# Two attention stages rebuilt: half steps, two PSUM rings, a mask product on TensorE

## The chip, the cores and the metric

The kernel runs as one program on one core of a Trainium2 chip. The metric is the time of one execution on the device in microseconds, lower is better. A profiled execution gives the trace from which the stages are read; its engines are PE (TensorE products), PEld (its weight loads), DVE (VectorE), ACT (ScalarE), POOL (GpSimd) and SP (the queue that issues most DMAs).

## What is computed

The input is eight sequences of 512 tokens with 128 features, in fp32. Twelve blocks follow one another, each with a residual connection and a layer norm in front: an LSTM-like block, a state-space mixer, the LSTM-like block again; a mixture of experts, attention L1, the mixture again; a gated block with rounded weights, a recurrence, the gated block again; a ReLU block, attention L3, the ReLU block again. This case is about the two attentions. Both have 16 heads of 8 features; L3 is causal:

```python
scores = jnp.einsum('bhqk,bhsk->bhqs', q, k) / jnp.sqrt(jnp.float32(dk))
causal_mask = jnp.triu(jnp.ones((s, s), dtype=bool), k=1)      # L3 alone
scores = jnp.where(causal_mask, jnp.float32(-1000000000.0), scores)
weights = jax.nn.softmax(scores, axis=-1)
ctx = jnp.einsum('bhqs,bhsk->bhqk', weights, v)
```

L1 adds position features to the normalized input ahead of the projections, adds that sum to its output, and normalizes once more with gamma and beta.

## The kernel before

Every stage works sequence by sequence; the eight sequences of x stay in SBUF for the whole run. `_run_stages` (L1307) calls the twelve stages in order. Within a stage the program text gives each engine its order, except where the scheduler of the tile framework moves instructions that are ready earlier; waits come from tiles: a tile of a ring with n buffers can be written again once the reader of the one n before it is done.

An attention stage (`attention`, L1002) is a pipeline over sequences:

- `project` (L1065): layer norm (statistics on DVE, the root on POOL, the application on ACT, L263), transposes, the products for q and k, each split in two fp32r halves (lead on ACT, trail on DVE), the products for v, and eight pairs of "spread" products that put the 8 features and both halves of a head on 32 rows: qT and kT of head group g hold four heads, 32 rows each.
- `maxima` (L1119): for each chunk c of 128 queries, each group and each head a product of 32 rows into one bank of the ring "mm" (three banks), whose negated row maximum DVE takes (L1146). In L3 a custom DVE instruction (L1135) adds the mask while it takes the maximum. 64 products and 64 DVE instructions per sequence. The maxima are then transposed and split in two halves (mT).
- `weighted` (L1168): 16 steps per sequence, one for each group g and chunk c of 128 keys. A step makes four products of keys by queries (32 rows each, scores transposed), and four more that add the negated maximum (max_rows by mT) in the same banks: two tiles of two banks, scores0 and scores1, one buffer each. ACT takes the exponential of each tile (L1223, 128 x 1024 values); in L3 the ranges are shorter (queries from chunk c on), and POOL clears what is above the diagonal in the first 128 queries (L1225). The value sums of the step before follow on PE: four products of 32 columns in one bank, "av", which fill the group's sums over its four chunks; v has a column of ones, so that the sum of weights comes with it.
- `fill` (L1162): products of zeros by ones into the bank of value sums, that add nothing: one per step in L1, c + 1 per step in L3.
- `attended` (L1241): transposes of the four ctx tiles, division, the output product, residual and (L1) the second norm, again applied on ACT.

In `weighted`, each step yields twice (room 3, then 2), and the loop at L1052 puts in between: `attended` of the sequence before, `project` of the next, then up to five maxima of the next sequence per step until they are done. The first sequence is projected and has its maxima taken ahead of all steps; the last one has none beside it. A stage begins with its constants (spread, zeros, ones, max_rows, mask, L1018 to L1039) and its weights, which `self.load(key)` (L1012) fetches on the SP queue into a tile that the mixer stage used before.

PSUM has eight banks: three of "mm", four of scores, one of "av". "mm" also serves all projections, transposes and output products.

Of the kernel before, what the change touches and what calls it, by code (L numbers as in the profile page):

```python
# [207 lines left out]

class _Kernel:
# [34 lines left out]
    def norm(self, x, pool, out=None, tag="xn", scalar=False):  # L244
# [26 lines left out]
        return xn  # L271

# [61 lines left out]
    def l0_attn(self):  # L334
# [8 lines left out]
        with ExitStack() as s:  # L343
# [58 lines left out]
            for _ in self.mixer_out(NB - 1):  # L402
                pass

# [216 lines left out]
    def l1_ffn(self):  # L621
# [3 lines left out]
        with ExitStack() as s:  # L625
# [3 lines left out]
            self.spread = keep.tile([P, 8, P], F32R, name="spread")  # L629
            nc.vector.tensor_copy(  # L630
                self.spread.rearrange("p e m -> p (e m)"), self.w["moe", "spread"]
# [4 lines left out]
            for b in range(NB):  # L636
                ahead = self.routed(b + 1) if b + 1 < NB else iter(())
                for _ in self.experts(b):
                    next(ahead, None)
                for _ in ahead:  # L640
                    pass
# [33 lines left out]
    def experts(self, b):  # L675
# [12 lines left out]
        for e in range(9):  # L688
# [7 lines left out]
            if e < 8:  # L696
                if e % 2 == 0:
                    pw = []
                    for k in range(e, e + 2):
                        r = bass.ts(k % 4, 32)  # L700
                        pw.append(ps.tile([P, L], F32, name="pw"))
                        self.mm(pw[-1], self.spread[r, k, :], q["shareT"][r, :])
                nc.vector.tensor_tensor(act, act, pw[e % 2], ALU.mult)  # L703
# [297 lines left out]

    def attention(self, key, causal):  # L1002
# [7 lines left out]

        nc, tc = self.nc, self.tc
        self.load(key)  # L1012
        with ExitStack() as s:
            keep = s.enter_context(tc.tile_pool(name="keep", bufs=1))
            sb = s.enter_context(tc.tile_pool(name="sb", bufs=2))
            ps = s.enter_context(tc.tile_pool(name="ps", bufs=3, space=bass.MemoryType.PSUM))
            self.key, self.causal, self.sb, self.ps = key, causal, sb, ps
            spread = keep.tile([P, 2, 2, 4, P], F32R, name="spread")  # L1018
            nc.gpsimd.memset(spread.bitcast(F32), 0.0)
            for g in range(4):  # L1020
                r = bass.ts(g, 32)
                nc.vector.tensor_copy(
                    spread[r, :, :, g, :],
                    self.w["heads", "spread"][r, :].rearrange("p (w h m) -> p w h m", w=2, h=2),
                )
            self.zeros = keep.tile([P, P], BF16, name="zeros")
            nc.gpsimd.memset(self.zeros, 0.0)
            self.ones = keep.tile([P, L], BF16, name="ones")
            nc.gpsimd.memset(self.ones, 1.0)
            max_rows = keep.tile([P, 4, P], F32R, name="max_rows")  # L1030
            nc.vector.tensor_copy(
                max_rows, self.w["heads", "max_rows"].unsqueeze(2).to_broadcast([P, 4, P])
            )
            self.spread, self.max_rows = spread, max_rows
            if causal:
                self.mask = keep.tile([P, L], F32, name="mask")
                nc.gpsimd.memset(self.mask, 0.0)
                nc.gpsimd.tensor_copy(self.mask[:, L - P :], self.w["const", "mask_qk"])
                self.unread = keep.tile([P, L], F32, name="unread")  # L1039
            self.seqs = [{} for _ in range(NB)]  # L1040
            for _ in self.project(0):
                pass
            for _ in self.maxima(0):
                pass
            for b in range(NB):
                between = []
                if b > 0:
                    between.append((self.attended(b - 1), False))
                if b + 1 < NB:
                    between.append((self.project(b + 1), False))  # L1050
                    between.append((self.maxima(b + 1), True))
                for room in self.weighted(b):  # L1052
                    if between:
                        gen, small = between[0]
                        for _ in range(room if small else 2):
                            if next(gen, gen) is gen:
                                between.pop(0)
                                break
                for gen, _ in between:
                    for _ in gen:  # L1060
                        pass
            for _ in self.attended(NB - 1):
                pass

    def project(self, b):  # L1065

        nc, sb, ps, key = self.nc, self.sb, self.ps, self.key
        w = lambda n: self.w[key, n]
        q = self.seqs[b]
        xn = self.norm(self.x[b], self.ln_pool, scalar=True)  # L1070
        if key == "l1a":
            xp = sb.tile([P, NC, D], F32, name="xp", bufs=3)
            nc.gpsimd.tensor_tensor(xp, xn, w("pe").rearrange("p (c d) -> p c d", c=NC), ALU.add)
            q["xp"] = xp
        else:
            xp = xn
        yield
        xT = self.transposed(xp, ps, sb.tile([P, L], F32, name="xT"), nc.scalar.copy)
        yield
        halves = {}  # L1080
        for n in ("q", "k"):
            pq = ps.tile([P, L], F32, name="mm")
            self.mm(pq, w("w" + n), xT)
            lead = sb.tile([P, L], F32R, name=f"{n}_lead", bufs=1)
            nc.scalar.activation(lead, pq, AF.Identity, bias=w("b" + n))
            trail = sb.tile([P, L], F32R, name=f"{n}_trail", bufs=1)
            nc.vector.scalar_tensor_tensor(
                trail, pq, w("b" + n), lead.bitcast(F32), ALU.add, ALU.subtract
            )
            halves[n] = (lead, trail)  # L1090
            yield
        v = sb.tile([P, NC, 9 * 16 + 23], F32, name="v")
        q["v"] = v
        nc.gpsimd.memset(v, 1.0)
        pv = ps.tile([P, NC, P], F32, name="mm")
        for c in range(NC):
            self.mm(pv[:, c, :], xT[:, bass.ts(c, P)], w("wv"))
        for c in range(NC):
            nc.vector.tensor_tensor(
                v[:, c, :144].rearrange("p (h e) -> p h e", e=9)[:, :, 0:8],  # L1100
                pv[:, c, :].rearrange("p (h e) -> p h e", h=16),
                w("bv").rearrange("p (h e) -> p h e", h=16),
                ALU.add,
            )
        yield
        q["qT"], q["kT"] = [], []
        for g in range(4):
            r = bass.ts(g, 32)
            for which, n in enumerate(("q", "k")):
                pq = ps.tile([P, L], F32, name="mm")  # L1110
                self.mm(pq, self.spread[:, which, 0, g, :], halves[n][0], stop=False)
                self.mm(pq, self.spread[:, which, 1, g, :], halves[n][1], start=False)
                t = sb.tile([P, L], F32R, name=f"{n}T{g}")
                nc.scalar.copy(t, pq)
                q[n + "T"].append(t)
            if g % 2:
                yield

    def maxima(self, b):  # L1119

        nc, sb, ps, causal = self.nc, self.sb, self.ps, self.causal
        q = self.seqs[b]
        mx = sb.tile([P, NC, 4, 4], F32, name="max")
# [207 lines left out]
```

## Time and profile before

| what | value |
|---|---|
| median of three runs | 2760.23 us (2742.91 to 2765.81) |
| the profiled execution | 2768.8 us, span 2767.0 us |
| L1 attention, first exponential to last sequence's start | 862 to 1362 us |
| L3 attention, the same | 2189 to 2650 us |
| mean granted TensorE clock | 0.892 |

The profile page gives for each engine the time in which it was busy, the span in 40 slices with the granted clock, and the costliest groups of instructions. A group's row holds line, engine and operation, output and inputs by tile name with shapes, then the count, busy time, mean duration in ns, and the idle time of that engine just before, with what ended it. A PE instruction counts as busy from issue to a modelled end, so starts are better to reckon with than ends. The busy times by stretch hold busy time and, in brackets, instructions of each engine. The timeline merges like instructions that follow one another; "[0.54 <-PE mm L242]" is 0.54 us of idle time that ended when that product was done. L242 is the line of the helper through which nearly all products go, so tiles tell them apart. An fp32 product is recorded as two instructions of two passes each; fp32r and bf16 products are one pass.

### The profile page before, as it was taken

How to read it: one execution, taken by the hardware profiler on the slowest of the kernel's cores; microseconds unless marked ns; L12 is line 12 of the kernel's file. 1: busy time of each engine (PE TensorE's matmuls, PEld its weight loads, DVE VectorE, ACT ScalarE, POOL GpSimd, SP SyncE). 2: the span in 40 equal slices, each digit the busy share in tenths (PEclk: the TensorE clock that was granted, in tenths of full speed). 3: DMA queues.
4: the chain of work that ended last, by engine and by line, in shares of the span. 5: the costliest groups of instructions: out<-in, count | busy, mean ns of one | idle time of the engine just before them, and what ended most of it. 6: DMA issues, size and time to landing. Idle time of an engine off the chain costs nothing.

```text
span 2767.0 us, 32181 instructions
## 1 busy us (share of the span) xinstructions
PE 2336.9 (84%) x10995; PEld 1110.9 (40%) x11087; DVE 1706.9 (62%) x4623; ACT 1334.9 (48%) x2247; POOL 644.4 (23%) x926
## 2 busy tenths in 40 slices
PE   7588998889989888888879996752779998999999
PEld 3434444434434333333334443431544444444434
DVE  4565654577767566666627777848863556656621
ACT  3288775323334665555543333474435244444444
POOL 1123233021120111111111114544542122222220
PEclk9598888999987999999989998975979699989989
DMA  3000000000000000000000000000000000000001
GB/s 106 0 1 1 1 1 12 9 1 0 1 0 1 1 1 1 1 1 1 1 6 0 1 1 1 1 1 0 1 1 1 0 1 1 1 1 1 1 1 31
DMA packets 10051, 13.20 MB, mean 5 GB/s; under 512 B 416, under 2 KB 8736, under 8 KB 9760
## 3 DMA queue, kind: packets, MB, share of 16 engines
q1 hardware_dynamic: 7776, 10.11, 1.1%
q8 instruction: 87, 1.43, 0.2%
q10 hardware_dynamic: 2112, 1.05, 0.1%
q14 instruction: 76, 0.62, 0.1%
HBM read 9.06 MB, written 2.10 MB: 4 GB/s over the span
## 4 chain that ended last, share of the span: by engine, by line
PE 60%; DVE 21%; ACT 8%; POOL 7%; issue 4%; DMA 0%; DVEq 0%; ACTq 0%; POOLq 0%; SPq 0%
PE mm L242 15%; PE av L242 10%; PE po L242 8%; DVE max L1146 6%; PE pg L242 5%; PE pu L242 5%; PE ck L242 4%; DVE unread L1135 3%; PE scores L242 3%; PE ph L242 2%; POOL xn_rstd L257 1%; PE pw L242 1%; ACT e L1223 1%; PE mm L277 1%; DVE xn L268 1%
## 5 line engine op out<-in xcount | busy, mean ns | idle before, releaser
L1223 ACT ACTIVATE e<-scores 128x1024 f32<-128x1024 f32 (+3 forms) x512 | 417.9, 863 | 310.3 <-PE scores L242 196.0
L242 PE MATMUL mm<-kT,qT 32*128 32x512 f32 (+3 forms) x1024 | 383.7, 479 | 71.8 <-DVE max L1146 29.4
L1146 DVE TENSOR_REDUCE max<-mm 128x1 f32<-128x512 f32 x512 | 315.4, 684 | 105.6 <-PE mm L242 102.1
L1135 DVE CUSTOM_DVE_ANT_0 unread<-mm,mask 128x512 f32<-128x512 f32 (+3 forms) x512 | 251.8, 492 | 158.5 <-PE mm L242 89.6
L242 PEld LDWEIGHTS mm<-kT,qT 32*128 32x128 f32 x1024 | 166.9, 198 | 289.5 <-DVE max L1146 153.1
L242 PE MATMUL av<-e,v 128*32 128x512 f32 (+3 forms) x2048 | 263.2, 539 | 1.8 <-issue 1.8
L242 PE MATMUL scores<-qT,kT 32*128 32x512 f32 (+3 forms) x1024 | 183.9, 438 | 13.3 <-ACT e L1223 10.0
L694 ACT ACTIVATE act<-pg 128x512 f32<-128x512 f32 x144 | 86.0, 597 | 220.9 <-PE pg L242 196.7
L1225 POOL TENSOR_SCALAR_AFFINE_SELECT e<-e 128x256 f32<-128x256 f32 x256 | 102.2, 406 | 294.0 <-ACT e L1223 291.5
L278 ACT COPY xT<-mm 128x512 f32<-128x512 f32 x112 | 65.2, 584 | 209.2 <-PE mm L277 205.2
L242 PE MATMUL po<-act,w_moe 128*128 128x512 f32 x288 | 159.0, 637 | 0.6 <-DVE act L703 0.6
L242 PE MATMUL pg<-xT,w_moe 128*128 128x512 f32 x288 | 155.7, 624 | 0.0
L242 PE MATMUL scores<-mT,max_rows 32*128 32x512 f32 (+3 forms) x1024 | 150.7, 385 | 0.0
L242 PE MATMUL pu<-xT,w_moe 128*128 128x512 f32 x288 | 149.2, 600 | 0.0
L695 DVE TENSOR_TENSOR act<-act,pu 128x512 f32<-128x512 f32 x144 | 98.3, 683 | 55.6 <-PE pu L242 53.6
L257 POOL TENSOR_TENSOR xn_rstd<-xn_rs,nhalf 128x4 f32<-128x4 f32 x96 | 104.3, 1088 | 87.1 <-ACT xn L263 53.9
L242 PE MATMUL av<-ones,zeros 128*128 128x512 bf16 x356 | 118.7, 414 | 5.3 <-issue 5.3
L1148 POOL COPY copies<-max 128x128 f32<-128x128 f32 x64 | 18.6, 291 | 448.9 <-DVE max L1146 361.6
L252 DVE BATCH_NORM_STATS2 xn_st<-x 128x6 f32<-128x128 f32 x384 | 96.2, 271 | 37.9 <-POOL x L1275 32.9
L242 PEld LDWEIGHTS <-zeros 128*128 128x128 bf16 x448 | 36.8, 100 | 174.8 <-issue 163.7
L242 PEld LDWEIGHTS scores<-qT,kT 32*128 32x128 f32 x1024 | 80.5, 191 | 53.4 <-ACT e L1223 27.8
L242 PE MATMUL mm<-xT,w_mixer 128*128 128x512 f32 (+1 forms) x176 | 94.1, 656 | 9.1 <-ACT xT L278 6.5
(327 smaller groups left out, 4482.8 us busy)
## 6 DMA issues: line engine op xcount, KB each, us to landing
w_moe<-in_moe SPq DMA_DIRECT2D x1, 2392.0 KB, 14.6
out<-x SPq DMA_DIRECT2D x8, 256.0 KB, 2.3
x<-in_u ACTq DMA_DIRECT2D x4, 256.0 KB, 6.3
x<-in_u SPq DMA_DIRECT2D x4, 256.0 KB, 6.4
w_mixer<-in_l0a SPq DMA_DIRECT2D x1, 954.5 KB, 8.2
w_mixer<-in_l1a SPq DMA_DIRECT2D x1, 769.0 KB, 4.1
w_ffn<-in_l0f SPq DMA_DIRECT2D x1, 578.0 KB, 7.3
w_ffn<-in_l2f SPq DMA_DIRECT2D x1, 560.0 KB, 3.4
```

The source lines that it names most:

```text
L242: self.nc.tensor.matmul(out, lhsT, rhs, start=start, stop=stop)
L252: nc.vector.bn_stats(st[:, c, :], x[:, c, :])
L257: nc.gpsimd.tensor_tensor(rstd, rs, self.nhalf[:, :n], ALU.pow)
L268: nc.vector.tensor_scalar(xn[:, c, :], x[:, c, :], mv[:, c, 0:1], rstd[:, c : c + 1], ALU.subtract, ALU.mult)
L277: self.nc.tensor.transpose(pt[:, c, :], xn[:, c, :], self.ident)
L278: copy(out, pt.rearrange("p c t -> p (c t)"))
L694: nc.scalar.activation(act, pg, AF.Silu)
L695: nc.vector.tensor_tensor(act, act, pu, ALU.mult)
L1135: nc.vector.tensor_tensor_reduce(self.unread[:, :n], sc[:, :n], self.mask[:, L - n :], scale=-1.0, scalar=-MASKED, op0=ALU.add, op1=ALU.mi ...
L1146: nc.vector.tensor_reduce(m, sc, AX.X, ALU.max, negate=True)
L1223: nc.scalar.activation(e[:, :, :n], sc[:, :, :n], AF.Exp, scale=scale)
L1225: nc.gpsimd.affine_select(e[:, :, :P], e[:, :, :P], pattern=[[0, 2], [1, P]], compare_op=ALU.is_ge, fill=0.0, base=0, channel_multiplier=-1,)
```

## The change

- **Half steps.** A step of four heads becomes two half steps of two heads: two score products, two max_rows products, one exponential. Their tiles come from a ring "pair" of two (two banks each), which also serves every transpose, projection and output product. The maxima have a ring of their own, "first", of three banks.
- **Fixed order.** Every half step issues exactly two maxima products of the next sequence (four are done ahead). All other pieces (norm in four parts, transposes, projections, spreads, output) are put after half steps whose numbers a table gives. Projections run two sequences ahead. In L1 PE keeps the written order by added dependencies without semaphores; the maxima products stand between scores and max_rows, on the rows that the scores do not use. In L3 they stand after max_rows, and the scheduler may move them.
- **Mask.** In L3 a product of a bf16 identity by a bf16 mask (128 rows, 128 columns) adds the mask in the bank, and DVE takes a plain maximum.
- **Value sums.** v is laid out as 32 columns per head with zeros; even groups use columns 0 to 8, odd ones 16 to 24, so two groups add up in one bank: two ctx tiles and eight transposes instead of four and sixteen.
- **The filling products are gone.**
- **Norms** in the attentions are applied on DVE instead of ACT.
- **Constants** are made once, in pieces, beside sequence 1 of the first mixture of experts, where DVE and POOL keep the written order; v's ones and zeros are written once in three tiles. The weights l1a are loaded at the end of the mixer stage, l3a at the end of L1.

The core of the diff:

```diff
+_SLOTS = {
+    "l1a": dict(
+        lead=4, attended=(4, 8, 10, 12, 13, 16, 17), spread=(0, 12, 12), turned=30,
+        projected=(3, 3, 5, 6, 12, 16, 18), spread0=20,
+    ),
+    "l3a": dict(
+        lead=4, attended=(8, 9, 10), spread=(2, 12, 16), turned=30,
+        projected=(3, 5, 7, 8, 14, 20, 20), spread0=22,
+    ),
+}
...
+            for _ in range(64 + _SLOTS[key]["lead"]):
+                next(maxima)()()
+            self.maxima_turned(0)
+            with self.in_order(*(() if causal else (mybir.EngineType.PE,))):
+                for b in range(NB):
+                    between = self.between(b)
+                    for at, step in enumerate(self.weighted(b)):
+                        step([m for m in (next(maxima, None), next(maxima, None)) if m])
+                        for piece in between.get(at, ()):
+                            piece()
+                self.product()
...
+    def pair(self):
+        return self.ps.tile([P, 2, L], F32, name="pair")
...
+    def spread_out(self, b, g):
+        q = self.seqs[b]
+        p = self.pair()
+        for k in range(2):
+            self.mm(p[:, k, :], self.spread[:, k, 0, g, :], q["lead"][:, k, :], stop=False)
+            self.mm(p[:, k, :], self.spread[:, k, 1, g, :], q["trail"][:, k, :], start=False)
+        t = self.sb.tile([P, 2, L], F32R, name=f"qkT{g}")
+        self.nc.scalar.copy(t, p)
...
+            sc = ps.tile([P, L], F32, name="first", bufs=3)
+            self.mm(
+                sc[:, :n], q["qT"][g][r, bass.ts(c, P)], q["kT"][g][r, :n], stop=not causal
+            )
+            if causal:
+                self.mm(sc[:, n - P : n], self.ident_bf, self.mask, start=False)
...
-                            nc.vector.tensor_tensor_reduce(
-                                self.unread[:, :n],
-                                sc[:, :n],
-                                self.mask[:, L - n :],
...
+                nc.vector.tensor_reduce(m, sc[:, :n], AX.X, ALU.max, negate=True)
...
-    def fill(self, out, n):
-        for _ in range(n):
-            self.mm(out, self.zeros, self.ones, start=False, stop=False)
...
+        if c == 0 and g % 2 == 0:
+            q["pav"] = self.ps.tile([P, L], F32, name="av", bufs=1)
+        for h in range(4):
+            self.mm(
+                q["pav"][bass.ts(h, 32), q0:],
+                q["v"][:, c, 4 * g + h, :],
+                es[h // 2][:, h % 2, : L - q0],
+                start=c == 0 and g % 2 == 0,
+                stop=c == NC - 1 and g % 2 == 1,
+            )
...
+        def half(g, c, pair, es, firsts):
+            sc = self.pair()
+            heads = (2 * pair, 2 * pair + 1)
+            for h in heads:
+                self.mm(
+                    sc[:, h % 2, :n], q["kT"][g][r, bass.ts(c, P)], q["qT"][g][r, q0:], stop=False
+                )
+            if not causal:
+                reads = [first() for first in firsts]
+            for h in heads:
+                self.mm(sc[:, h % 2, :n], self.max_rows[r, g, :], q["mT"][r, q0:], start=False)
+            if causal:
+                reads = [first() for first in firsts]
+            e = sb.tile([P, 2, L], F32, name="e", bufs=6)
+            nc.scalar.activation(e[:, :, :n], sc[:, :, :n], AF.Exp, scale=scale)
...
+            for read in reads:
+                read()
+            if pair == 1:
+                self.product()
+                self.unmultiplied = (q, g, c, es)
```

## The prediction

> **What bounds the kernel now.** I read the page first, then the busy times by stage, then the timeline of single steps. The page:
>
> ```profile
> span 2767.0 us, 32181 instructions
> ...
> PE 2336.9 (84%) x10995; PEld 1110.9 (40%) x11087; DVE 1706.9 (62%) x4623; ACT 1334.9 (48%) x2247; POOL 644.4 (23%) x926
> ...
> PEclk9598888999987999999989998975979699989989
> ...
> L1146 DVE TENSOR_REDUCE max<-mm 128x1 f32<-128x512 f32 x512 | 315.4, 684 | 105.6 <-PE mm L242 102.1
> L1135 DVE CUSTOM_DVE_ANT_0 unread<-mm,mask 128x512 f32<-128x512 f32 (+3 forms) x512 | 251.8, 492 | 158.5 <-PE mm L242 89.6
> ...
> L242 PE MATMUL av<-ones,zeros 128*128 128x512 bf16 x356 | 118.7, 414 | 5.3 <-issue 5.3
> ```
>
> PE is busy most, but DVE's maxima wait about 100 us for PE in each attention, and PE waits for them too: a loop between two engines, not one full engine. Now the stages (columns: stretch, length, busy PE, PEld, DVE, ACT, POOL, then the granted clock). L1 attention runs from 800 to 1432, L3 from 2128 to 2698.
>
> ```profile
> 862.00:1362.00 500.00, 430.18 (x2705) 177.77 (x2745) 328.12 (x661) 293.91 (x371) 60.76 (x86) 0.96 0.00 1
> 1362.00:1432.00 70.00, 55.18 (x340) 21.86 (x344) 10.96 (x44) 40.77 (x51) 11.98 (x13) 0.86 0.01 1
> ...
> 2189.00:2650.00 461.00, 419.05 (x2877) 191.66 (x2918) 268.08 (x1055) 212.25 (x352) 116.39 (x276) 0.92 0.00 1
> 2650.00:2698.00 48.00, 42.70 (x351) 19.48 (x355) 7.43 (x26) 24.74 (x40) 15.59 (x35) 1.00 0.01 1
> ```
>
> The first and third stretches hold seven sequences each: 71.4 us per sequence in L1, 65.9 in L3. In L1 DVE works 46.9 of the 71.4 and ACT 42.0. One step (a group of four heads and a chunk of keys) of L1:
>
> ```profile
> 1043.34 3.08 DVE L1146 TENSOR_REDUCE max<-mm 128x1 f32<-128x512 f32 x5 [0.54 <-PE mm L242]
> ...
> 1043.86 1.94 ACT L1223 ACTIVATE e<-scores 128x1024 f32<-128x1024 f32 x2 [1.66 <-PE mm L242]
> ...
> 1044.68 0.18 PEld L242 LDWEIGHTS mm<-kT,qT 32*128 32x128 f32 x1 [0.42 <-DVE max L1146]
> 1045.10 0.16 PEld L242 LDWEIGHTS av<-e,v 128*32 128x32 f32 x8 [0.24 <-issue]
> ...
> 1046.10 0.10 PEld L242 LDWEIGHTS <-zeros 128*128 128x128 bf16 x1 [0.84 <-issue]
> ...
> 1046.42 0.18 PEld L242 LDWEIGHTS mm<-kT,qT 32*128 32x128 f32 x2 [0.23 <-DVE max L1146]
> ```
>
> The step is 3.62 (1042.80 to 1046.42): five maxima at 0.60 and 0.54 of idle DVE, because PE, in order, does value sums (1.00) and a filling product (0.32) before it comes back to maxima. About 13 of 16 steps look so; three have no maxima and take 2.61, as at 1395 to 1403. That makes 54.9, and 16.5 of the 71.4 go to the pieces between. One cause of these:
>
> ```profile
> 1374.42 1.65 ACT L263 ACTIVATE yn<-o,yn_off,yn_rstd 128x128 f32<-128x128 f32 x4 [3.44 <-DVE yn_off L261]
> 1375.97 1.91 ACT L1223 ACTIVATE e<-scores 128x1024 f32<-128x1024 f32 x2
> ...
> 1377.03 0.79 PE L242 MATMUL scores<-qT,kT 32*128 32x512 f32 x2 [3.87 <-ACT e L1223]
> ```
>
> A normalization waits on ACT for its statistics and holds the exponentials; PE idles 3.87 and the clock halves. It halves about once per sequence. In L3 it halves without that:
>
> ```profile
> 2416.00:2420.00 4.00, 3.45 (x29) 1.50 (x26) 3.18 (x12) 0.66 (x2) 0.77 (x2) 0.93 0.00 0
> 2420.00:2424.00 4.00, 3.64 (x17) 1.72 (x17) 2.54 (x9) 1.79 (x2) 0.41 (x1) 0.50 0.00 0
> ...
> 2436.00:2440.00 4.00, 3.31 (x19) 1.34 (x14) 1.44 (x5) 0.75 (x2) 0.37 (x2) 0.50 0.00 0
> ```
>
> About 72 of the 461 us of L3 are at half clock, with PE busy over 80%.
>
> **The change, part by part.** The sum is against the profiled execution, 2768.8 us (span 2767.0 and 1.8 around it); the median of the runs shown, 2760.2, is 8.6 lower, and I take that off at the end.
>
> *L1, steady sequences.* A pass of 512 columns takes 0.21 at full clock (fp32 records, two passes each, start 0.43 apart). Call the issue of two maxima products 0. DVE starts at 0.54 and ends at 1.14 and 1.74. The other half step's second product needs the slot freed at 1.14 (three slots), so it issues at 1.20 and ends at 1.43 with the max_rows on other rows beside it; 0.21 to switch to value sums (the 0.42 above less one pass) and 1.00 for them: the next two products issue at 2.64. Data come at 3.18, DVE was done at 2.94, ACT needs 1.94. So 2.64 a step, 42 for 16. The pieces: four spreads at 0.95, q and k 1.75, values and output 0.9 each, transposes 2.7, about 10 of PE; eleven switches at 0.2; half step 12 takes three slots of the pair ring, whose two copies (0.97 each, as an e row) stand before the next scores: 2; at the end of a sequence the last maximum, POOL's copy, transposes, ACT's copy and DVE's subtraction precede the first max_rows, with one half step as cover: about 2, less what overlaps: 14 in all, against 16.5 now. The ACT wait of 3.44 goes with the normalization's move to DVE; late next is the PE piece itself, behind which scores and so ACT queue. 56 a sequence: 7 x (56 - 71.4) = -108. Bounds: only the filling goes, 16 x 0.32 = 5.1, so -36; or DVE alone bounds, 46.9 and eight applications at 0.28 (1.11 for four), 49.1, so -156. I take the value in between because the chain is made of rows of this stage.
>
> *L1, last sequence.* Without maxima a step is now 2.61: 1.94 of ACT and a 0.67 gap, since all four heads' scores wait for both exponentials. In half steps one pair is filled while the other is read; PE needs four passes, switches and value sums, 2.15: 16 x 0.46 = 7, and the stall of 1374 with its slow clock, 6: -13 (bounds -5 and -20).
>
> *Preparation.* Before L1's first exponential (800 to 862) the constants go from DVE (2.14 and 4.97) and POOL, but four more maxima (2.4) and the second sequence's projections (about 4 of DVE) come in: 0, from -5 to +8. In the first l1_ffn the constants add 7 of DVE and 8 of POOL in one sequence; DVE is busy 165 of 224 there, so most hides behind PE: +3, from 0 if all hides to +10 if none. The loads move on SP's queue: now l1a issues at 476.5, l2f at 541.5, l3a at 1430.9; afterwards l2f stands behind l3a, at about 1310, and is used first after the second l1_ffn: nothing, covered by that stage; without the cover its landing, 3.4.
>
> *Fewer pieces of a kind.* Two copies of value sums (0.58) instead of four, 8 transposes instead of 16, no memset of v (0.65 to 0.92, POOL): in the terms above.
>
> *L3's mask on TensorE.* DVE's 0.645 per maximum (means of 0.44, 0.58, 0.71, 0.85 start to start by width) becomes a reduction of about 0.40 (the 0.60 row, scaled in columns): DVE drops to some 32 per sequence and no longer matters. PE pays: 64 mask products of 128 rows among products of 32 rows. No row shows that pair; the nearest are 32-row product to value sums or to filling (0.42 start to start, 0.21 over the pass) and filling to 32-row product (0.32, 0.10 over). So 0.21 + 0.05 + 0.10 = 0.36 each at full clock; at half clock the same rows are 0.72 and 0.54, which gives 0.52. Bounds: 0.05, the pass alone, and 0.52. Per group: scores 1.07, max_rows with one maxima product beside them 1.39, the other product 1.07, masks 16 x 0.36 = 5.6, value sums 2.5: 11.6, 46 per sequence and 12 of pieces: 58. At half clock 20.1 a group and 22 of pieces: 102. How much runs slow? I take a fifth, near the 15% now: the filling (10 products a group) goes, the mask's full rows come. 58 + 0.2 x 44 = 67: 7 x (67 - 65.9) = +8; bounds -55 (never slow) and +253 (always).
>
> *The rule that speaks against it.* The Trainium skill, "TensorEngine Tiling (Array Packing)", Key Properties, says that changing the tiling mode drains TensorE; it gives no time, so the sum by it is the one by the rows above. "TensorE: Matmul & The Clock Gate", in its goals, asks only that PE have no idle gaps over about 3 us; by that the filling could go free, L3 would stay fast, and the sum would be lower by 63. The rows at 2420 speak against it, and I go by the rows.
>
> *L3, rest.* Before the first exponential maxima were DVE's (64 x 0.645 = 41); 68 products with masks at half clock take PE 0.27 + 0.52 each, 54: +12 with the projections against the constants (0 to +20). Last sequence, no mask in it: 16 steps of about 1.6 instead of 2.1: -8 (0 to -12).
>
> Sum: -108 - 13 + 0 + 3 + 8 + 12 - 8 = -106, so 2663 against the profiled execution, 2654 as a median.
>
> **The rivals.** (1) L3 falls to half clock for most of its time: the light chunks have neither filling nor wide scores. It speaks for this that 2420 happened even with filling; against it, that the pieces (spreads, q and k) are now spread over the sequence and each dense one brings the clock back, as at 2446. Slower than before from 55% slow work, where 7 x (44f - 7.9) eats the other -114; at three quarters 2822. (2) L3 never slow: -55 for +8, 2591. (3) L1 stays tied: PE, now in strict order, stands in the pieces as before and only the filling is won: -36 for -108, 2726. (4) L1 reaches DVE's bound: -156, 2606.
>
> **How the numbers follow.** Forecast 45%, (1) 20%, (2) 13%, (3) 12%, (4) 10%. Range 2560 to 2800: below, (2) and (4) in part together; above, (1) up to about 70% slow. The forecast's own range is 2610 to 2700. A measurement of this kernel tells about 1% from no change. Faster by over 1% (below 2733): the forecast, (2), (4) and half of (3), rounded for doubt in the forecast, 0.72; (3)'s rest and the mild end of (1), 0.12 the same; the rest of (1), 0.16 slower.
>
> **What would show it.** L1's steady stretch at 54 to 58 per sequence, steps near 2.64, no wait of ACT for yn_off, clock at 0.96 or more. Mask to next 32-row product and back at 0.36. L3 at about 67 per sequence, clock 0.85 to 0.95. I am wrong if the L1 step stays above 3.2, if L3's clock is below 0.75, or if PE does not bound L3.

## The result and the profile after

The changed kernel takes 2836.91 us (median of four runs, 2834.62 to 2841.14) against 2760.39 for the kernel before: a ratio of 1.029, interval 1.0242 to 1.0338. It is slower; the forecast was 2654, with a range to 2800. The profiled execution has a span of 2833.0, 66.0 more than before. From the page after:

```profile
span 2833.0 us, 30824 instructions
...
PE 2467.4 (87%) x11023; PEld 1191.6 (42%) x11023; DVE 1705.8 (60%) x4068; ACT 1294.6 (46%) x2055; POOL 649.1 (23%) x914
...
PEclk9598888999977999998999896698855655555569
...
L1264 DVE TENSOR_REDUCE max<-first 128x1 f32<-128x512 f32 (+3 forms) x1024 | 567.9, 587 | 395.1 <-PE first L255 392.9
...
L255 PE MATMUL first<-mask,ident_bf 128*128 128x128 bf16 x512 | 140.4, 274 | 0.0
```

In the row of the clock, L1 (slices 14 to 18) runs at 9; L3 (slices 30 to 39) lies at 5 and 6, where the kernel before had mostly 8 and 9. PE is busy 130 us longer with 28 more instructions, and DVE waits 395 us ahead of the maxima of the two attentions, where it waited 264 (105.6 in L1, 158.5 in L3). By stage (columns as before; the first stretch holds L1's seven steady sequences, the second its last sequence, then L3's preparation, its steady sequences, its last one):

```profile
867.00:1265.00 398.00, 356.49 (x2580) 143.93 (x2582) 325.70 (x599) 277.63 (x295) 54.09 (x72) 0.96 0.00 1
1265.00:1321.00 56.00, 46.52 (x317) 19.77 (x313) 10.31 (x33) 35.57 (x39) 10.98 (x11) 0.91 0.00 1
2029.00:2088.00 59.00, 58.60 (x171) 29.69 (x172) 39.22 (x84) 5.61 (x7) 2.91 (x6) 0.57 0.00 0
2088.00:2712.00 624.00, 621.84 (x3024) 299.83 (x3020) 255.17 (x569) 208.84 (x295) 115.99 (x270) 0.58 0.00 1
2712.00:2763.00 51.00, 44.73 (x302) 20.39 (x299) 4.89 (x12) 23.81 (x37) 14.51 (x34) 0.70 0.00 1
```

The kernel before, cut in the same way, from the first exponential to that of the last sequence (L3; in L1 it is 862 to 1365; the prediction's stretches were 3 us shorter):

```profile
2189.00:2653.00 464.00, 421.89 (x2894) 193.50 (x2935) 270.49 (x1063) 212.83 (x353) 116.68 (x277) 0.92 0.00 1
```

L1's steady sequences take 398 instead of 503: 56.8 each, the gain that was forecast. L3's take 624 instead of 464, 89.1 each instead of 66.3. In these 624 us PE is without work for 2, DVE is busy 255 and ACT 209: PE alone bounds L3, at a granted clock of 0.58, which is half clock for 85% of the time (15% before). One step of L1 in the timeline after, weight loads left out:

```profile
1149.81 2.48 DVE L1264 TENSOR_REDUCE max<-first 128x1 f32<-128x512 f32 x4 [0.27 <-PE first L255]
1150.07 2.15 ACT L1341 ACTIVATE e<-pair 128x1024 f32<-128x1024 f32 x2 [0.61 <-PE pair L255]
1150.56 0.50 PE L255 MATMUL first<-qkT 32*128 32x512 f32 x1 [0.36 <-DVE max L1264]
1150.56 0.50 PE L255 MATMUL pair<-mT,max_rows 32*128 32x512 f32 x2
1150.99 1.07 PE L255 MATMUL av<-e,v 128*32 128x512 f32 x8
...
1152.56 0.69 DVE L1264 TENSOR_REDUCE max<-first 128x1 f32<-128x512 f32 x1 [0.27 <-PE first L255]
```

From one DVE start to the next: 2.75 a step, 2.48 of it four maxima. The forecast was 2.64. And PE in L3:

```profile
2399.62 0.52 PE L255 MATMUL pair<-mT,max_rows 32*128 32x384 f32 x2
2400.07 0.29 PE L255 MATMUL first<-mask,ident_bf 128*128 128x128 bf16 x1
2400.28 0.58 PE L255 MATMUL first<-qkT 32*128 32x256 f32 x1
2400.79 0.29 PE L255 MATMUL first<-mask,ident_bf 128*128 128x128 bf16 x1
2401.01 1.94 PE L255 MATMUL av<-e,v 128*32 128x512 f32 x8
2402.88 0.58 PE L255 MATMUL pair<-qkT 32*128 32x256 f32 x2
```

No row shows a wait. A mask product and a maxima product take turns, and each start stands 0.2 to 0.5 behind the last, at half clock (value sums of 1.94 for 1.07 in L1).

### The profile page after: what moved, and what is told of

Read it like the earlier page. It is cut to its first block, busy times and chain, and to the rows that moved or that the text cites. A ratio compares the mean times of both kernels' runs of the same rounds, so it can differ in the third digit from the quotient of the medians.

```text
span 2833.0 us, 30824 instructions
## 1 busy us (share of the span) xinstructions
PE 2467.4 (87%) x11023; PEld 1191.6 (42%) x11023; DVE 1705.8 (60%) x4068; ACT 1294.6 (46%) x2055; POOL 649.1 (23%) x914
## 4 chain that ended last, share of the span: by engine, by line
PE 66%; DVE 15%; ACT 8%; POOL 6%; issue 3%; DMA 0%; ACTq 0%; SPq 0%; DVEq 0%; POOLq 0%
PE pair L255 14%; PE first L255 12%; PE av L255 9%; PE po L255 7%; PE pg L255 4%; PE pu L255 4%; PE ck L255 3%; PE mm L255 3%; DVE max L1264 3%; PE ph L255 2%; ACT e L1341 2%; POOL xn_rstd L270 1%; DVE xn L281 1%; PE pw L255 1%; PE pf L255 1%
## 5 line engine op out<-in xcount | busy, mean ns | idle before, releaser
L1264 DVE TENSOR_REDUCE max<-first 128x1 f32<-128x512 f32 (+3 forms) x1024 | 567.9, 587 | 395.1 <-PE first L255 392.9
L1341 ACT ACTIVATE e<-pair 128x1024 f32<-128x1024 f32 (+3 forms) x512 | 438.9, 864 | 446.7 <-PE pair L255 436.6
L255 PE MATMUL first<-qkT 32*128 32x512 f32 (+3 forms) x1024 | 474.8, 555 | 24.8 <-DVE max L1264 23.9
L255 PE MATMUL pair<-qkT 32*128 32x512 f32 (+3 forms) x1024 | 261.5, 531 | 19.8 <-ACT e L1341 14.4
L255 PEld LDWEIGHTS first<-qkT 32*128 32x128 f32 x1024 | 206.7, 229 | 110.0 <-DVE max L1264 70.8
L255 PEld LDWEIGHTS pair<-qkT 32*128 32x128 f32 x1024 | 112.0, 220 | 296.3 <-issue 132.5
L255 PE MATMUL pair<-mT,max_rows 32*128 32x512 f32 (+3 forms) x1024 | 218.6, 434 | 1.0 <-DVE mT L1287 1.0
L255 PE MATMUL first<-mask,ident_bf 128*128 128x128 bf16 x512 | 140.4, 274 | 0.0
L1266 POOL COPY copies<-max 128x128 f32<-128x128 f32 x64 | 26.3, 411 | 432.1 <-DVE max L1264 431.4
L255 PEld LDWEIGHTS pair<-mT,max_rows 32*128 32x128 f32 x1024 | 120.3, 238 | 1.9 <-DVE mT L1287 1.7
L769 DVE TENSOR_TENSOR act<-act,pw 128x512 f32<-128x512 f32 x128 | 87.1, 682 | 16.5 <-PE pw L255 15.0
```

The lines of the kernel that those rows point to most:

```text
L255: self.nc.tensor.matmul(out, lhsT, rhs, start=start, stop=stop)
L1264: nc.vector.tensor_reduce(m, sc[:, :n], AX.X, ALU.max, negate=True)
L1266: nc.gpsimd.tensor_copy(copies[:, :, :, :, g], mx[:, g].unsqueeze(3).to_broadcast([P, NC, 4, 8]))
L1341: nc.scalar.activation(e[:, :, :n], sc[:, :, :n], AF.Exp, scale=scale)
```

## The experiments

The first theory, A, was rival 1 of the prediction: the filling has gone, so PE's array has too little to do and the clock stays at half. The rival, B: the mask products, with their changes between 32 and 128 rows, are what takes the clock away, or are the cost themselves. The table has the median time of each kernel and, from its one profiled execution, L3's seven steady sequences. "Changes" counts neighbouring products of different rows or columns. "Work" is an estimate from the records: each product's passes of 512 columns at the 0.213 us that such a pass takes at full clock, times the share of the 128 x 128 array that its rows and columns use.

| kernel | total us | us a sequence | at half clock | changes | work |
|---|---|---|---|---|---|
| before | 2760 | 66.3 | 15% | 64 | 31.3 |
| after | 2837 | 89.1 | 85% | 145 | 26.3 |
| e1 no mask in the maxima | 2557 | 52.8 | 37% | 52 | 23.0 |
| e2 mask on DVE | 2615 | 60.6 | 61% | 52 | 23.0 |
| e3 filling back | 2688 | 68.3 | 2% | 152 | 33.1 |
| e4 wide masks | 2663 | 65.5 | 9% | 138 | 30.5 |
| e5 as e1, a filling product a step | 2544 | 51.6 | 12% | 67 | 26.3 |
| e6 as e2, filling back | 2581 | 55.1 | 2% | 67 | 31.4 |
| e7 before, no filling | 2726 | 67.7 | 46% | 56 | 24.1 |
| e12 masks in pairs | 2557 | 50.7 | 4% | 84 | 26.3 |
| e13 as e5, thin steps only | 2536 | 48.0 | 6% | 59 | 24.6 |
| e14 as e13, strict order | 2541 | 52.9 | 29% | 57 | 24.7 |
| e15 as e12, two slots | 2667 | 66.5 | 38% | 98 | 26.3 |
| e16 as e12, strict order | 2555 | 50.5 | 2% | 80 | 26.4 |

**e1: no mask in L3's maxima.**

```diff
-            if causal:
-                self.mm(sc[:, n - P : n], self.ident_bf, self.mask, start=False)
```

> This kernel leaves the mask out of L3's maxima (the maximum is taken over the chunk's whole last 128 keys, which is still an upper shift of the softmax; the exponentials are masked as ever). So 64 mask products per sequence and their switches go. Theory A (L3 is slow because PE's array is too little used and the clock stays at half): the clock stays low, each mask product saves its cold price of 0.41, L3 goes from 89 to about 64 per sequence and the time to about 2665 us, with a granted clock in L3 still below 0.75. Rival B (the mask products and their switches are themselves what is slow and what costs the clock): the clock comes back, L3 goes to 39 to 46 per sequence and the time to about 2530 us.

Measured 2557.28 (0.9277, 0.9229 to 0.9324). The line of L3's steady sequences:

```profile
2064.00:2433.00 369.00, 350.19 (x2583) 175.75 (x2579) 232.62 (x570) 200.84 (x295) 115.07 (x270) 0.81 0.00 1
```

Between the two and nearer to B. The clock is neither back nor at half.

**e2: the mask on DVE again.** The edit of e1, and in L3:

```diff
-                nc.vector.tensor_reduce(m, sc[:, :n], AX.X, ALU.max, negate=True)
+                nc.vector.tensor_tensor_reduce(self.unread[:, :n], sc[:, :n], self.maskf[:, L - n :], ...)
```

> The mask goes back to DVE (0.65 a maximum instead of 0.57), everything else of the changed kernel stays, no filling. Theory A: PE has the same work as without any mask, at half clock it is the bound and DVE hides (42 of some 64 per sequence): about 2670 us, granted clock in L3 below 0.75. Rival B: the clock comes back and DVE bounds L3 at 46 to 50 per sequence: about 2550 us.

Measured 2614.79 (0.9464, 0.9435 to 0.9492), clock 0.69: in between again.

```profile
2074.00:2498.00 424.00, 406.80 (x2581) 201.31 (x2585) 261.60 (x1019) 202.90 (x296) 115.35 (x270) 0.69 0.00 1
```

PE's products and changes are those of e1, only DVE is slower, and yet half clock grows from 37% to 61%. Neither the work of a sequence nor its changes can explain that.

**e3: filling back in L3, mask kept on TensorE.**

```diff
+        if causal and c < NC - 1:
+            for _ in range(c + 1):
+                self.mm(q["pav"], self.zeros, self.ones, start=False, stop=False)
```

(for the last chunk it stands ahead of the value sums, as before)

> The filling products of the kernel before (one to four per step, onto the bank of value sums) are put back in L3 alone; the mask stays on TensorE. Theory A: the clock comes back to 0.85 or more in L3, and though PE has 40 products more per sequence (9 us at full clock) L3 goes from 89 to about 70 per sequence: about 2700 us. Rival B: the masks still cost what they cost, the filling comes on top, 9 to 17 per sequence: 2900 us or more.

Measured 2687.67 (0.9725, 0.9694 to 0.9757), as A has it: 40 more products a sequence, and 20.8 us less.

```profile
2087.00:2565.00 478.00, 464.47 (x3245) 230.17 (x3296) 248.94 (x569) 206.63 (x295) 115.25 (x270) 0.99 0.00 1
```

**e4: every mask product as wide as its maxima product.**

```diff
-                self.mm(sc[:, n - P : n], self.ident_bf, self.mask, start=False)
+                self.mm(sc[:, :n], self.ident_bf, self.maskw[:, L - n :], start=False)
```

> Each mask product is made as wide as its maxima product (128 to 512 columns, zeros but for the last 128), with the same number of products and of switches: 12288 columns of full-array work more per sequence, against 20480 that the filling has. Theory A: the clock comes up, to about 0.75 in L3, and L3 falls to about 75 per sequence in spite of 5 us more work at full clock: about 2740 us. Rival B: 5 to 10 us per sequence more: 2870 to 2910 us.

Measured 2662.58 (0.9637, 0.96 to 0.9673), better than A forecast.

```profile
2097.00:2555.00 458.00, 449.83 (x2993) 217.95 (x3024) 254.36 (x569) 206.72 (x295) 115.39 (x270) 0.95 0.00 1
```

The number of mask products is unchanged, the changes are 138 against 145, each product is longer, and L3 is 23.6 us a sequence faster. B's form, that the changes take the clock, falls here.

**e5: e1 with one filling product a step.** The edits of e1 and e3, with `range(1)` for `range(c + 1)`.

> As the run without a mask in L3's maxima (the maximum is over the whole last 128 keys of the chunk), with one filling product of 512 columns put into each step of L3. That run still spent stretches at half clock (0.81 granted over its steady sequences, 369 us for seven). Theory A (the clock follows the array's work): 16 products of 0.22 cost 3.5 a sequence, the clock goes to 0.95 or more, and every sequence takes the 48 that the undisturbed ones nearly take: 340 for seven, about 2530 us. Rival (one small product per step is too little, or the clock's stretches have another cause): 370 to 395 for seven, 2557 to 2580 us.

Measured 2544.48 (0.9217, 0.919 to 0.9243), L3's clock 0.94, between the two expectations: six of seven sequences at 47.8 to 53.0; the first, 59.3, still starts at half clock.

**e6: e2 with the old filling.** The edits of e2 and e3 together.

> L3's mask on DVE as in the kernel before and its filling too (one to four products per step); rings, half steps, grouped value sums and placed pieces of the changed kernel stay. Theory A: clock 0.95 or more; PE needs the 69 of the filled kernel less 64 mask products of 0.30, so 49.5, DVE some 47: about 51 a sequence, 357 for seven against 425 without filling: about 2550 us. Rival (DVE bounds the kernel with the mask on it, and its filling adds to it): 61 a sequence or more, 2615 us or more.

Measured 2580.64 (0.9347, 0.9321 to 0.9374), clock 0.99, 55.1 a sequence: the filling alone brings e2 34 us, as A has it, though not quite its 51. With mask and filling as in the kernel before, the new rings, half steps and placed pieces make L3 faster by 11.2 a sequence, of which some 7 remain when both times are multiplied by their clock (66.3 x 0.92 and 55.1 x 0.99); the rest is the clock.

**e7: the kernel before without filling.**

```diff
-        for _ in range(n):
+        for _ in range(0):
             self.mm(out, self.zeros, self.ones, start=False, stop=False)
```

> The kernel before with no filling product in either attention. In L1 each step loses 0.32: 71.4 becomes about 66 a sequence, if the clock holds as it does in the changed kernel's L1 (0.96). In L3, theory A: the clock falls to 0.6 to 0.75 and eats what the 40 products gave back: 64 to 70 a sequence as against 66; about 2730 us in all. Rival B (the clock of L3 doesn't hang on the filling, the mask products alone took it): L3 gains the 9 of the products, 57 a sequence at a clock of 0.9: about 2670 us.

Measured 2725.8 (0.987, 0.9833 to 0.9907). L1 goes from 71.9 to 65.7; L3 stays at 67.7 with its clock down from 0.92 to 0.77. So without any mask on PE the filling was already what held L3's clock.

**e8: one filling product a step back in L1 of the changed kernel.**

```diff
+        if not causal and c < NC - 1:
+            for _ in range(1):
+                self.mm(q["pav"], self.zeros, self.ones, start=False, stop=False)
```

> The changed kernel with one filling product per step put back in L1 alone. If PE's order is the path of L1's step, as the prediction has it, the 16 products come on top with 0.22 to 0.32 each: 56.8 becomes 60.5 to 62 a sequence and the time about 2870 us. If PE has slack there, nothing changes: 2837 us. L3 is untouched.

Measured 2869.85 (1.039, 1.0347 to 1.0433); L1 61.1 a sequence. The product lies on L1's path at 4.3 a sequence, 0.27 a step.

**e9: the changed kernel without the strict order of PE in L1.**

```diff
-            with self.in_order(*(() if causal else (mybir.EngineType.PE,))):
+            with self.in_order():
```

> The changed kernel without the strict order of PE in L1: the scheduler may then pull maxima products ahead and split the value sums. If L1's gain of 15 a sequence comes from the separate rings, the half steps and the missing filling, as the prediction's chain has it, L1 stays at 56 to 58 a sequence: 2837 to 2850 us. If it is the strict order that made it, L1 goes back toward the 66 of the kernel before without filling: 2890 us or more. L3 is untouched.

Measured 2865.75 (1.038, 1.0343 to 1.0417); 58.9 a sequence in the profiled execution, 21 us more in L1 as a whole. Between the two: the order is worth 2 of the 15 a sequence, the rest of L1's gain does not need it.

**e10: the kernel before, its attentions' normalizations on DVE.**

```diff
-        xn = self.norm(self.x[b], self.ln_pool, scalar=True)
+        xn = self.norm(self.x[b], self.ln_pool)
...
-            yn = self.norm(y, self.ln_pool, tag="yn", scalar=True)
+            yn = self.norm(y, self.ln_pool, tag="yn")
```

> The kernel before with only the normalizations of its attentions moved from ACT to DVE. If ACT's wait for the statistics (3.44 at 1374, once or twice a sequence, with a stretch of slow clock behind it) is on the path of L1, 3 to 6 a sequence go there: 2735 to 2750 us. If it is hidden anyway, the eight applications of 0.28 come onto DVE, which stands in a loop with PE: the same to 2 a sequence slower, 2760 to 2785 us.

Measured 2757.31 (0.9989, 0.9971 to 1.0008): the same. Steady L1 goes from 71.9 to 72.8; only the last sequence, with no maxima on DVE, falls from 48.7 to 41.3: 6.3 us lost in seven sequences, 7.4 won in one. The wait shown at 1374 belongs to that last sequence, and there alone it was on the path.

**e11: two slots instead of three for the maxima.**

```diff
-            sc = ps.tile([P, L], F32, name="first", bufs=3)
+            sc = ps.tile([P, L], F32, name="first", bufs=2)
```

> The changed kernel with two slots instead of three in the ring of maxima. The prediction's chain for L1 lets a half step's second product issue when the slot of the third reduction before it is freed; with two slots it waits for the reduction just before it, and PE, in strict order, with it: the step goes from 2.75 to 3.4 to 3.6 and L1 from 56.8 to 66 to 70 a sequence: 2900 to 2930 us, little in L3, where PE and not DVE bounds. If the slots don't matter: 2837 us.

Measured 2933.75 (1.0633, 1.0595 to 1.0671); L1 64.5 a sequence, L3 92.5. The third slot of the maxima's own ring is worth 7.7 a sequence in L1, less than the 9 to 13 expected, and 3.4 in L3, where little was expected.

**e12: the masks in pairs.** A half step issues both maxima products, then both mask products (the mask product has become a function of its own, which the cut leaves out).

```diff
             if causal:
                 reads = [first() for first in firsts]
+                for mask, _ in reads:
+                    mask()
```

> The changed kernel with the two maxima products of a half step first and their two mask products behind them: the same products, half the changes between 32 and 128 rows in L3. Theory A: array work is unchanged, the clock stays at half for most of L3, and only the changes are saved, 0.3 a pair: 10 a sequence, about 2770 us. Rival B (the changes themselves bring the clock down): the clock comes back to 0.8 or more, L3 goes to about 58 to 62 a sequence, about 2630 us.

Measured 2557.2 (0.9271, 0.9242 to 0.9301), 50.7 a sequence, far below A and below B.

```profile
2085.00:2440.00 355.00, 348.06 (x3019) 180.84 (x3018) 235.25 (x569) 202.99 (x295) 115.43 (x270) 0.98 0.01 1
```

The timeline of PE in e12, one half step:

```profile
2260.71 0.38 PE L255 MATMUL pair<-qkT 32*128 32x256 f32 x2
2260.72 0.32 PE L255 MATMUL first<-qkT 32*128 32x128 f32 x1
2260.93 0.28 PE L255 MATMUL pair<-mT,max_rows 32*128 32x256 f32 x2
2260.96 0.32 PE L255 MATMUL first<-qkT 32*128 32x128 f32 x1
2261.22 0.29 PE L255 MATMUL first<-mask,ident_bf 128*128 128x128 bf16 x2
2261.43 0.85 PE L255 MATMUL av<-e,v 128*32 128x384 f32 x8
```

Scores and maxima of different rows start 0.01 apart, max_rows and the second maximum 0.03, and the value sums 0.21 after the first of the two masks. With this run A falls as it was stated: the work of 26.3 is that of the changed kernel, and the clock is back. Of the 38.4 us a sequence between the two kernels (89.1 and 50.7), about 8 are the changes themselves and about 30 the clock; that is an estimate, from the 59 that the changed kernel would take at full clock by e3 (worked out below).

**The theory after that, C: work per time.** Changes of the clock stand whole multiples of 3.41 us apart in the traces, so I cut L3 of fifteen kernels (the changed one and its variants) into such windows and summed the estimated work in each. Of 1000 windows at full clock with at least 0.38 of what the whole array could do at full clock, none was followed by half clock; of 128 with less, 71 were. At half clock 70 windows of 877 reached 0.37 (0.74 of what half clock allows), and 55 of these were followed by full clock; of the other 807, 23. One line, 0.37, tells the next window's clock in 1930 of 2005 windows. Most windows just keep their clock: it changed after 149 (71, 55 and 23), so "no change" alone would be right in 1856. Rows alone (counting each product as full in columns) leave 490 wrong, the time in which any product streams 108, work 75. The counts take in the four runs that follow; the line itself was set before them, as e13's expectation shows.

Windows outside the 2005 are a harder trial. In L1 of seven kernels (before, after, e7 to e11; 914 windows) the line is wrong 14 times, "no change" 62. In L3 of the kernel before, e7 and e10 (403 windows) it is wrong 65 times, "no change" only 55, and a line at 0.415 of the time in which any product streams (counted in granted clock) 38. One half held everywhere: of these windows at full clock, 803 in L1 and 218 in L3 had at least 0.38, and none was followed by half clock. The other half did not: in that L3 only 28 of the 85 with less were. So these traces show that enough work keeps the clock. Where too little loses it, and whether work or streaming time is the better measure, is not settled; no run was made to separate them.

The time lost at a change counts as no work, so C takes the part of B that was right: pairs of masks shorten the step and so raise the work per time; wide masks raise the work itself. By C a low clock also holds itself down: at half clock the same chain does less per window, so only a dense stretch such as spreads and projections comes over the line. Four more runs followed: e13 and e15 to try C, e14 and e16 on PE's order.

**e13: e1 with a filling product in the thin steps only.** As e5, but:

```diff
-        if causal and c < NC - 1:
+        if causal and c == 2:
```

> As the run without a mask in L3's maxima and with one filling product a step, but the filling only in the two thin steps of each group (chunks 2 and 3, 256 and 128 columns): 8 products a sequence instead of 16. Theory C (the clock goes by the array's work per time in windows of 3.4 us; at full clock the windows with more than 0.37 of the array's capacity were never followed by the slow clock): the thin steps are where the windows fall below, so the clock stays at 0.93 or more and L3 gains 8 x 0.22 = 1.8 a sequence, 49 to 50: about 2532 us. Rival: the wide steps need it as well, the clock falls to 0.8 to 0.85 and L3 takes 52 to 53: 2550 to 2557 us.

Measured 2535.55 (0.9185, 0.9135 to 0.9235), near C's 2532. The clock of 0.97 and the 48.0 a sequence are those of the profiled execution, which was the fastest of four (2514.53; the others 2532.49 to 2547.96, with a granted clock of 0.883 to 0.892 over the whole run for 0.901). In the others L3 was probably slower, so the clock did not always hold as C has it, and the slowest comes near the rival's 2550. It has the lowest median of the study, not told apart from e14's; its maxima take in keys that the mask would leave out.

```profile
2064.00:2400.00 336.00, 316.87 (x2638) 156.40 (x2632) 231.47 (x570) 199.51 (x295) 114.76 (x270) 0.97 0.00 1
```

**e14: e13 with PE's strict order in L3.**

```diff
-            with self.in_order(*(() if causal else (mybir.EngineType.PE,))):
+            with self.in_order(mybir.EngineType.PE):
```

> The same kernel with PE held to the order of emission in L3 too. If the scheduler's own order in L3 splits value sums and maxima as it does in L1 (where the strict order was worth 2 to 5 a sequence), L3 gains 2 to 4 a sequence, about 2515 us; if DVE's or ACT's waits stand in the strict order, it loses 1 to 3 a sequence, about 2545 us.

Measured 2540.87 (0.9214, 0.9184 to 0.9244), not told apart from e13, so no gain from the order; the second expectation, 2545, is the nearer. In the profiled execution four sequences take 48.3 to 49.7, the others up to 59.0, and half clock has 29% of the time: with half the filling the thin windows lie at the line (stretches of slow clock began after windows of 0.27 to 0.37). That this execution has 29% and e13's has 6% is the spread between executions, since the medians are 5 us apart.

**e15: e12 with two slots instead of three in L3.**

```diff
-            sc = ps.tile([P, L], F32, name="first", bufs=3)
+            sc = ps.tile([P, L], F32, name="first", bufs=2 if causal else 3)
```

> The kernel with grouped masks (2557 us, clock 0.98 in L3's steady sequences, 50.7 each), with two slots instead of three in L3's ring of maxima: the same products and the same changes of rows, only more waiting of PE for DVE. Theory C: the waiting takes the thin steps under 0.37, the clock falls, at half clock the work per time can't come back over it, and L3 goes to 75 a sequence or more: 2720 us or more. Rival B (the number of changes between 32 and 128 rows sets the clock): it stays at 0.95, the waiting itself costs 3 to 8 a sequence: 2580 to 2615 us.

Measured 2667.48 (0.9662, 0.9632 to 0.9693).

```profile
2087.00:2552.00 465.00, 457.12 (x3020) 229.08 (x3013) 241.26 (x570) 205.74 (x295) 116.27 (x270) 0.81 0.00 1
```

The same products, and the clock falls from 0.98 to 0.81, in 17 stretches, most of which end at dense pieces; four end behind windows with 0.19 to 0.24 of work and no such piece, which C does not explain. C had the direction, but too long a stay (75 a sequence for 66.5). The scheduler also moves products here, 98 changes for 84, so it isn't waiting alone that differs.

**e16: e12 with PE's strict order in L3.** The edit of e14 on e12.

> The kernel with grouped masks, PE held to the order of emission in L3 too. The emission already has the order in which scores, maxima, masks and max_rows stand, so I expect little: 50 to 52 a sequence, 2550 to 2565 us, with the clock still at 0.95 or more. If the strict order makes PE wait in L3 for pieces or for DVE, the thin steps fall under 0.37 and the clock goes: 2650 us or more.

Measured 2554.58 (0.9262, 0.9245 to 0.928), clock 0.99: as expected, the order changes little.

```profile
2087.00:2440.00 353.00, 336.71 (x3024) 176.58 (x3024) 236.51 (x571) 203.99 (x296) 115.60 (x270) 0.99 0.01 1
```

It and e12 compute all that the kernel before does. By e12 the changed kernel needed its mask products in pairs, and nothing else, to be faster by 7%.

## Why the prediction was wrong, point by point

| term (us) | forecast | measured |
|---|---|---|
| L1, steady sequences | -108 | -105.6 |
| L1, last sequence | -13 | -9.6 |
| constants and L1's preparation | +3 | +5.3 |
| from L1 to L3's first maximum | 0 | -2.0 |
| L3, preparation | +12 | +10.9 |
| L3, steady sequences | +8 | +159.5 |
| L3, last sequence | -8 | +7.6 |
| sum | -106 | +66.0 |

The measured terms are differences of the two profiled executions between first maximum, first exponential, last sequence's first exponential and last sum of x; they add up to the 66.0 of the spans to 0.1.

**L1 was right.** The step is 2.75 for 2.64, a sequence 56.8 for 56, the clock 0.96. With all 16 steps at 2.75 the forecast had the steps 1.8 a sequence too cheap and the pieces (12.8 for 14) 1.2 too dear; that the two nearly cancel is luck. The third slot (e11, 7.7) and the filling (e8, 4.3) each show on the path. One reason in this term was wrong: moving ACT's wait for the normalization to DVE won the steady sequences nothing (e10: 71.9 to 72.8), it won in the last one, where I had it too, at 6; e10 shows 7.4. The loads on SP's queue and the preparations came out as costed, to 3 us.

**The mask's price was right.** Start to start and over the pass of the maxima product, the change to the mask costs 0.20 at full clock and 0.30 at half, and the next product starts 0.16 and 0.22 after the mask: 0.36 and 0.52, as forecast. (In e1's expectation I had taken 0.41 for half clock, which was too low. And in the forecast 16 masks at 0.36 make 5.8 a group and not 5.6, 0.6 a sequence more.) The ends of the mixture were near: L3 at full clock, forecast 58, comes out of e3 as 59 (68.3 times its clock of 0.99 is 67.5, less 40 products of 0.22), and the slowest sequences take 93.7 to 93.9 (e8 and e11), still at a clock of 0.55; none with all its pieces ran at half clock from end to end, for which I had 102.

**The step that failed** is "How much runs slow? I take a fifth". At a granted clock of 0.58, 85% of the time is slow. By the prediction's own formula 89.1 = 58 + 44 f makes f 0.71, so rival 1, at three quarters 2822, is what happened; it had 20%. The runs show the size of the step: with the filling back (e3) the same products and 40 more take 68.3 a sequence at a clock of 0.99, with the masks in pairs (e12) they take 50.7 at 0.98, and the kernel before, without its filling, goes from 15% to 46% of slow time (e7). What misled me was to take the old share of slow time as an anchor, and to weigh the dense pieces as if each won back the time after it. The trace after shows that each win was short: in L3 the clock came back after 7 of 154 slow windows, stayed for some four windows on the mean, and fell again behind windows that held 0.30 to 0.34. The rows at 2420, which I quoted, were a sign of a line, and the question to ask was on which side of it the new step lies: 26.3 of work in 58 us is 0.45 on the mean, where the kernel before had 31.3 in 61.2 us (66.3 times its clock of 0.92), 0.51.

**The rules weighed.** I went by the rows and against the Trainium skill, "TensorE: Matmul & The Clock Gate", whose goals ("Why this matters for your kernels") ask that PE have no idle gaps over about 3 us. That was right: PE is without work 2 of 624 us and L3 is slow, and e3 makes PE's work longer and L3 faster. The same page, Part 1, gives a free-running window of 3413 ns, and the traces agree (all changes at whole multiples of 3.41); what counts in it is, by the runs here, not the engine's busy time of the profile; the work of the array follows the clock better, with the limits told under C. That a change of tiling mode drains TensorE ("TensorEngine Tiling (Array Packing)", Key Properties) agrees with the 0.20 of a change above, and the page has no price; what the changes did to the clock, by fewer products per window, was dearer (about 30 of the 38 a sequence in e12's estimate).

**L3's last sequence** missed its sign for the same cause: it ran at 0.70 instead of 1.00.

What stays open: the line of 0.37 rests on an estimated work, its 75 exceptions aren't explained, and in L3 of the kernel before it fails; whether work or streaming time sets the clock; whether e15's loss is waiting alone or also its changes of order was not separated.

## What to carry to other kernels

Where PE bounds a stage, count its work per time: the columns that its products stream, times the share of the array that they fill, over the time that the step takes at full clock, in the thinnest 3.4 us and not on the mean. Here the clock held in every window with 0.38 or more. Where a step lies near that, filling is not waste, and a small product between products of another shape costs twice, in its own switch and in the clock; put products of one shape together, or make them wider. An old share of slow time says nothing of a new step: work out on which side of the line it comes to lie.

## What the runs showed that I had not expected

- More work made the stage faster: 40 filling products a sequence took L3 from 89.1 to 68.3, mask products two and a half times as wide on the mean to 65.5.
- The order of four products decided 280 us: maxima and masks in turns 2837, in pairs 2557, with the same work of the array.
- The clock did not go by how long PE was busy: at a busy share of 99.7% PE was granted 0.58, and with 95% busy in e16 0.99. How much of the array was at work in 3.41 us tells it better.
- A normalization whose wait showed 3.44 us of idle ACT and 3.87 of idle PE brought nothing when it was moved (0.9989): the row stood in the one sequence that has DVE free, which won 7.4, and the seven others lost 6.3.
